# Scores and mix of an attention block by seven half-block products, with sums kept in PSUM

## The chip, the cores and the metric

The kernel runs on one core of a Trainium2 chip. The metric is the device time of one execution in microseconds (us). A core has TensorE (PE; the loads of its weights are shown apart as PEld), VectorE (DVE), ScalarE (ACT), GpSimd (POOL) and SyncE (SP, which only issues transfers). Each engine works through its own queue in order. TensorE writes its results to PSUM, eight banks of 128 x 512 float32.

## The reference, cut to what matters

There are four sequences of 512 tokens by 512 features, all in float32, with full 512 x 512 attention and no mask:

```
q, k, v  = x @ Wq, x @ Wk, x @ Wv
attn     = softmax(q @ k.T * 512**-0.5)
attn_out = (attn @ v) @ Wp + bp
cms      = gelu(attn_out @ cW1 + cb1) @ cW2 + cb2 + one_hot(code)
mod      = gelu(concat(attn_out, cms) @ mW1 + mb1) @ mW2 + mb2
y        = clip(x + cms + mod, 0, 1)
# then, per sequence, an adapter chosen by its stream:
out      = layernorm(y + gelu(y @ Wd + bd) @ Wu + bu) * g + b
```

cW1 is 512 x 2048, mW1 1024 x 2048, cW2 and mW2 2048 x 512, Wd 512 x 256.

## The kernel before

Everything is kept with features (or the summed index) on the 128 partitions. A tile of 512 x 512 is four chunks of 128 x 512. The sequences are worked on in two pairs. First an **attention stage** runs for both pairs; then, for each pair, the layers c1 (cW1), c2 (cW2), m1 (mW1), m2 (mW2) and the adapters follow.

The attention is folded. `block_weights` makes `w_qk` = Wq Wk^T and `w_vp` = Wv Wp once. For a pair, the loop does the following:

- `transposed` turns the rows of x (16 transposes of 128 x 128 on TensorE into four banks) to get `xT`.
- `pair_product` with `w_qk` makes `u` for both sequences at once. It is a Strassen-Winograd product: each operand is cut into four blocks, and seven block products of sums of blocks take the place of eight. The two sequences are the two column blocks of the right operand, so a block product has 512 columns. Each product lands in a bank of its own, and VectorE adds it to the running results in SBUF (`plus`, `add`, line 512).
- `softmax` makes the **scores** of each sequence, `u`^T `xT`, as a plain product: 4 row tiles of 4 chained products of 512 columns (line 596). Per tile VectorE takes the maximum, ScalarE the exponential with its sum, VectorE the reciprocal, ScalarE scales.
- The probabilities are turned (line 414), and `product` makes the **mix** of each sequence, again plain (line 428). `second_operand` forms the sums of blocks that the next pair product needs while it empties the banks.
- `pair_product` with `w_vp` and the bias makes `attn`, which the ACT queue sends to memory (`attn_kept`, line 647).

A float32 product is two matmul instructions in the profile, each with its own weight load.

The operand sums of the weights of c1, c2, m1 and m2 are made by GpSimd during the attention stage and the first c1 layer (`expansion`, called in steps from the loop). The c1 layer takes its seven outer products in the order 2, 1, 5, 6, 7, 3, 4; products 1 and 5 are themselves cut into seven (`inner`, called from `c1_layer`, line 787), with ScalarE copying the first product (line 680) and VectorE doing seven additions into SBUF for each half `g` of the rows (line 673). The weights come over SP's queue (`fetch`, line 762) into four places, `wslot[0]` to `wslot[3]`, taken in turn by `next_weights`. Ahead of them on that queue stands `load_attn` (line 732), which brings the first pair's `attn` back into the slots that held `x_rows[2]` and `x_rows[3]`.

A framework orders the instructions of each engine: by the order of the program, but an instruction whose inputs it takes to be late can be passed by a later one. `keep_in_program_order` forbids that for one instruction. It also hands out the PSUM banks (`bank`, eight in all); a product waits until one is free.

Of the kernel before, what the change touches and what calls it, by code (L numbers as in the profile page):

```python
# [18 lines left out]
def kernel(  # L19
# [452 lines left out]
    transposed(chunks(x_rows[0]), big[2])  # L472
    load_bias()
# [47 lines left out]

    def second_operand(v0, v1, space):


        t12, t34 = (t.rearrange("p (k c) n -> p k c n", k=2) for t in space)
        t1, t2, t3, t4 = t12[:, 0], t12[:, 1], t34[:, 0], t34[:, 1]

        def minus(out_, one, two):
            nc.vector.tensor_tensor(out_, one, two, ALU.subtract)

        def finish(d, ps):
            nc.scalar.copy(v1[:, d, :], ps)
            c = d % 2
            if d < 2:
                minus(t1[:, c], ps, v0[:, c, :])
            else:
                minus(t2[:, c], ps, t1[:, c])
                minus(t3[:, c], ps, v1[:, c, :])
            if d == 3:
                minus(t4, v0[:, 2:4, :], t2)  # L540

        operands = {
            1: v0[:, 0:2, :], 2: v0[:, 2:4, :], 3: v1[:, 2:4, :], 4: t4, 5: t1, 6: t2, 7: t3,
        }
        return operands, finish

    def pair_product(lhs, rhs, out, bias_c=None):

        p5 = [None, None]
        for p in (1, 2, 5, 6, 7, 3, 4):  # L550
            for r in range(2):
                c11, c12, c21, c22 = (out[k][:, o + r, :] for o in (0, 2) for k in range(2))

                def plus(dst, ps, other, o):
                    if bias_c is None:
                        add(dst, ps, other)
                    else:
                        nc.vector.scalar_tensor_tensor(
                            dst, ps, bias_c[:, o + r : o + r + 1], other, ALU.add, ALU.add
                        )  # L560

                ps = bank(f"pair{p}")
                for c in range(2):
                    nc.tensor.matmul(  # L564
                        ps,
                        lhsT=lhs[p][:, c, r * P : (r + 1) * P],
                        rhs=rhs[p][:, c, :],
                        start=(c == 0),
                        stop=(c == 1),
                    )  # L570
                if p == 1:
                    nc.scalar.copy(c11, ps)
                    nc.scalar.copy(c21, ps)
                elif p == 2:
                    plus(c11, ps, c11, 0)
                elif p == 5:
                    p5[r] = ps
                elif p == 6:
                    add(c21, ps, c21)
                    add(c12, p5[r], c21)  # L580
                elif p == 7:
                    plus(c21, ps, c21, 2)
                    add(c22, p5[r], c21)
                elif p == 3:
                    plus(c12, ps, c12, 0)
                else:
                    add(c21, ps, c21)
# [3 lines left out]
    def softmax(k, xT, u):  # L591
        rows = []
        for t in range(NT):
            ps = bank("scores")
            for c in range(NV):
                nc.tensor.matmul(  # L596
                    ps,
                    lhsT=u[:, c, t * P : (t + 1) * P],
                    rhs=xT[:, c, :],
                    start=(c == 0),  # L600
                    stop=(c == NV - 1),
                )
            top = small.tile([P, 1], F32, name="top")
            nc.vector.tensor_reduce(top, ps, AX.X, ALU.max)
            low = small.tile([P, 1], F32, name="low")
# [672 lines left out]
```

## Time and profile before

| | |
|---|---|
| median of three runs | 1213.1 us (1208.37, 1213.10, 1213.13) |
| the profiled execution | 1209.13 us, its span in the trace 1207.3 us |
| attention stage in the trace | 0 to about 264 us |
| first pair's c1 layer | about 264 to 358 us |
| PE busy, share of the span | 1183.2 us, 98% |
| DVE | 866.9 us, 72% |
| ACT | 226.1 us, 19% |
| POOL | 460.8 us, 38% |
| granted TensorE clock | 0.997 of full speed |

How to read the profile: "busy" of an engine is the time in which at least one of its instructions was open. A matmul's duration overlaps that of the next, so its mean duration is longer than its share: the time from one matmul to the next is read from the chain that ended last, where a run of them is one piece with its count. That chain follows the work back from the end, at each step to what released it; the names in it are engine, tile written and line. A group line gives the line, engine, operation, output and inputs, count, busy time, the mean of one in ns, and, after the bar, the idle time of the engine just before these instructions with what ended it.

### The profile page before, as it was taken

The page shows a single profiled execution, that of the slowest core. Times are in us where ns is not written, and L with a number is a line of the kernel's source. Part 1 is how long each engine was busy: PE and PEld are TensorE (multiplying, and loading weights), DVE is VectorE, ACT ScalarE, POOL GpSimd, SP SyncE. Part 2 cuts the span into 40 slices and gives each one's busy share as a digit, 9 for nine tenths or more (in the row PEclk, how much of TensorE's full clock was granted, in tenths as well). Part 3 has the DMA queues.
Part 4 walks back from the last instruction along what each step waited for, and adds up shares of the span by engine and source line. Part 5 has one row for each costly group of instructions (what it writes and reads, how often), then busy time and mean ns, then how long its engine had stood idle before and what let it go on. Part 6 is the DMA issues. An engine that isn't in the chain of part 4 may idle for free.

```text
span 1207.3 us, 12428 instructions
## 1 busy us (share of the span) xinstructions
PE 1183.2 (98%) x4593; PEld 853.5 (71%) x4593; DVE 866.9 (72%) x1156; ACT 226.1 (19%) x383; POOL 460.8 (38%) x501
## 2 busy tenths in 40 slices
PE   8999999999999999989999999999999999999996
PEld 5444454447458888878888857547888888888872
DVE  2542453167979876899799938879895578699947
ACT  3132114104130000003220025332000003230014
POOL 6679999979700028980000443200000010124015
PEclk9999999999999999999999999999999999999998
DMA  9656575797734667876756563233654555674601
GB/s 332 260 192 243 191 298 207 265 372 269 248 118 175 244 227 295 332 277 202 234 204 239 185 226 96 87 106 130 249 169 142 207 183 190 202 252 179 230 1 70
DMA packets 78364, 251.46 MB, mean 208 GB/s; under 512 B 7348, under 2 KB 34016, under 8 KB 63456
## 3 DMA queue, kind: packets, MB, share of 16 engines
q1 hardware_dynamic: 54768, 149.96, 34.9%
q0 software_dynamic: 20736, 89.17, 21.0%
q10 hardware_dynamic: 2800, 11.54, 2.4%
q8 instruction: 36, 0.59, 0.2%
q14 instruction: 24, 0.20, 0.0%
HBM read 185.63 MB, written 65.01 MB: 208 GB/s over the span
## 4 chain that ended last, share of the span: by engine, by line
PE 91%; DVE 4%; issue 3%; POOL 1%; DMA 0%; ACT 0%; ACTq 0%; DVEq 0%; POOLq 0%
PE i L977 28%; PE i L893 26%; PE c L829 11%; PE pair L564 8%; PE prod_ps L428 7%; PE scores L596 5%; PE i L787 2%; PE down_ps L1085 2%; PE tr_ps L414 1%; DVE hidden L512 1%; PE up_ps L1097 1%; DVE slot L190 1%; POOL part L1080 1%; DVE part L673 0%; POOL part L1130 0%
## 5 line engine op out<-in xcount | busy, mean ns | idle before, releaser
L893 PE MATMUL i<-slot,wslot 128*128 128x256 f32 x1184 | 261.6, 379 | 3.8 <-DVE part L673 3.8
L893 PEld LDWEIGHTS i<-slot,wslot 128*128 128x128 f32 x1184 | 224.6, 190 | 35.5 <-DVE part L673 4.1
L977 PE MATMUL i<-slot,wslot 128*128 128x256 f32 x896 | 202.5, 379 | 0.0
L977 PEld LDWEIGHTS i<-slot,wslot 128*128 128x128 f32 x896 | 170.2, 190 | 23.1
L977 PE MATMUL i<-hidden,wslot 128*128 128x256 f32 x576 | 132.2, 379 | 0.0
L680 ACT COPY first<-i 128x256 f32<-128x256 f32 (+1 forms) x56 | 26.8, 478 | 542.3 <-PE i L977 280.6
L673 DVE TENSOR_TENSOR part<-i,part 128x512 f32<-128x512 f32 (+1 forms) x156 | 90.9, 591 | 42.4 <-PE i L893 25.8
L977 PEld LDWEIGHTS i<-hidden,wslot 128*128 128x128 f32 x576 | 109.4, 190 | 16.2 <-issue 1.4
L702 ACT ACTIVATE hidden<-hidden,bias 128x512 f32<-128x512 f32 x128 | 85.2, 714 | 113.9 <-DVE hidden L512 112.0
L829 PE MATMUL c<-slot,wslot 128*128 128x512 f32 x224 | 96.9, 592 | 0.0
L829 PEld LDWEIGHTS c<-slot,wslot 128*128 128x128 f32 x224 | 42.6, 190 | 53.6 <-issue 50.7
L1048 POOL DMA_INDIRECT slot<-in_L_cond_b_up,idx_e x3 | 4.3, 1424 | 187.7 <-PE i L893 187.0
L1048 POOL DMA_INDIRECT slot<-in_L_cond_W_down,idx_d x12 | 15.5, 1291 | 149.8 <-PE i L977 88.6
L673 DVE TENSOR_TENSOR hidden<-i,hidden 128x512 f32<-128x512 f32 x80 | 53.6, 685 | 13.1 <-PE i L893 12.1
L512 DVE TENSOR_TENSOR hidden<-hidden,hidden 128x512 f32<-128x512 f32 (+2 forms) x48 | 58.9, 1231 | 1.2
L284 POOL DMA_DIRECT2D slot<-in_L_cond_mW x24 | 17.9, 761 | 107.6 <-DVE slot L190 106.6
L190 DVE TENSOR_TENSOR slot<-hidden,slot 128x1024 f32<-128x1024 f32 x48 | 58.4, 1218 | 0.3
L190 DVE TENSOR_TENSOR slot<-hidden 128x1024 f32<-128x1024 f32 x48 | 58.4, 1217 | 0.0
L673 DVE TENSOR_TENSOR part<-i,first 128x512 f32<-128x512 f32 (+1 forms) x62 | 36.3, 589 | 27.8 <-PE i L893 15.4
L512 DVE TENSOR_TENSOR hidden<-part,hidden 128x2048 f32<-128x2048 f32 x20 | 55.7, 2784 | 0.5
L512 DVE TENSOR_TENSOR hidden<-c,hidden 128x512 f32<-128x512 f32 x64 | 43.3, 685 | 16.8 <-PE c L829 16.1
L596 PE MATMUL scores<-hidden,hidden 128*128 128x512 f32 x128 | 55.3, 592 | 0.0
(270 smaller groups left out, 1793.6 us busy)
## 6 DMA issues: line engine op xcount, KB each, us to landing
wslot<-m_kept SPq DMA_DIRECT2D x48, 1024.0 KB
wslot<-m_kept SPq DMA_DIRECT2D x36, 512.0 KB
wslot<-c_kept SPq DMA_DIRECT2D x16, 1024.0 KB
slot<-in_L_cond_mW POOLq DMA_DIRECT2D x24, 512.0 KB
wslot<-in_L_cond_mW SPq DMA_DIRECT2D x24, 512.0 KB
slot<-in_L_cond_cW POOLq DMA_DIRECT2D x16, 512.0 KB
wslot<-in_L_cond_cW SPq DMA_DIRECT2D x32, 256.0 KB
m_kept<-wide POOLq DMA_DIRECT2D x6, 1024.0 KB
```

The source lines that it names most:

```text
L190: i = eng.tensor_tensor(out_, one, two, ALU.subtract)
L428: nc.tensor.matmul(ps, lhsT=lhs(c)[:, d * P : (d + 1) * P], rhs=rhs(c), start=(c == 0), stop=(c == 3),)
L512: nc.vector.tensor_tensor(dst, a, b, ALU.add)
L564: nc.tensor.matmul(ps, lhsT=lhs[p][:, c, r * P : (r + 1) * P], rhs=rhs[p][:, c, :], start=(c == 0), stop=(c == 1),)
L596: nc.tensor.matmul(ps, lhsT=u[:, c, t * P : (t + 1) * P], rhs=xT[:, c, :], start=(c == 0), stop=(c == NV - 1),)
L673: nc.vector.tensor_tensor(dst, ps, other, ALU.add)
L680: nc.scalar.copy(c1, p1)
L702: nc.scalar.activation(block[:, t, :], block[:, t, :], AF.Gelu, bias=bias_c[:, 8 * half + t : 8 * half + t + 1],)
L787: nc.tensor.matmul(out_ps[:, j, :], lhsT=a[:, place[q], j * P : (j + 1) * P], rhs=two_level[p][q][:, 0, :], start=True, stop=True,)
L829: nc.tensor.matmul(ps, lhsT=lhs(c, t), rhs=one_level[p][:, c, :], start=(c == 0), stop=(c == 1),)
L893: nc.tensor.matmul(out_ps[:, j, :], lhsT=a[j][q][:, c, :], rhs=now[q][:, c, :], start=(c == 0), stop=(c == 1),)
L977: nc.tensor.matmul(ps[:, :256], lhsT=a[k // 2][q][:, k % 2, :], rhs=now[q][:, k, :], start=(k == 0), stop=(k == 3),)
```

## The change

1. **Scores and mix** become seven block products each (`small_product`): both operands of 512 x 512 are cut into four blocks of 256 x 256, and a block product is 2 row tiles x 2 chunks of 256 columns in one bank.
2. **Sums left in PSUM** (`seven`, used by the scores, the mix, the pair products and the inner products of c1): products 2, 7, 4 and 3 are added by TensorE onto a bank that already holds an earlier product or a sum that VectorE wrote there. Per row tile, ScalarE (for the first mix VectorE) copies product 1 out, VectorE forms 1+5 in SBUF and three sums in PSUM, and ScalarE copies each finished block out; in the pair product with the bias it adds the bias in the same instruction.
3. **Operand sums**: each left operand needs s1 to s4 and each right operand t1 to t4, of 128 x 2 x 256 each. They are made on VectorE, in part while banks are emptied (`right_from_psum`, `beside_u`), in part by pinned instructions called after a given block product (`later`, `then`). They lie in `wslot[0]` to `wslot[2]` and in parts of `big` not in use; `wslot[3]` holds the copies of product 1 and the sums 1+5.
4. **Turning beside products**: the turning of Wv, of both sequences' probabilities and of the second pair's x is issued after a given block product inside another product.
5. The softmax works on 256 rows x 512 keys as two blocks: two maxima of 128 x 2 x 256, one small maximum, four exponentials of 256 columns with their sums, and the scaling. The scale of the maximum moves from VectorE to ScalarE; `constants` moves from behind the weight product of the first pair to behind its last pair product.
6. In the c1 layer, products 1 and 5 take both halves `g` side by side (two weight tiles at once), with their temporaries in `mod[0]`; h11 is added to straight from PSUM, and its eight gelus follow product 5. The generator of the layer pauses 12 times instead of 14.

The diff, cut to its core:

```diff
--- before
+++ after
-    transposed(chunks(x_rows[0]), big[2])
-    load_bias()
...
+        def take(half, at, ps):
+            c, n = at
+            into_ = slice(2 * half + c.start, 2 * half + c.stop)
+            nc.scalar.copy(v1[:, into_, n], ps)
+            if half == 0:
+                minus(t1[:, c, n], ps, v0[:, into_, n])
             else:
-                minus(t2[:, c], ps, t1[:, c])
-                minus(t3[:, c], ps, v1[:, c, :])
-            if d == 3:
-                minus(t4, v0[:, 2:4, :], t2)
+                minus(t2[:, c, n], ps, t1[:, c, n])
+                minus(t3[:, c, n], ps, v1[:, c, n])
+        last = later((t4, v0[:, 2:4, :], t2, ALU.subtract))
...
-    def pair_product(lhs, rhs, out, bias_c=None):
...
+    def seven(rows, matmuls, keep, order, then=None, copy=nc.scalar.copy, at=None):
+        w, x, y, c1, c15 = ([None] * rows for _ in range(5))
+        def space():
+            temps[0] += 1
+            k = temps[0] % 4
+            return wslot[3][:, 512 * k : 512 * k + 512] if at is None else at[:, k, :]
+        for p in order:
+            for r in range(rows):
+                if p in (1, 5, 6):
+                    ps = bank(f"sum{p}")
+                    {1: w, 5: y, 6: x}[p][r] = ps
+                else:
+                    ps = {2: w, 7: x, 4: x, 3: y}[p][r]
+                matmuls(p, r, ps, p in (1, 5, 6))
+                if p == 1:
+                    c1[r] = space()
+                    copy(c1[r], ps)
+                elif p == 5:
+                    c15[r] = space()
+                    add(c15[r], ps, c1[r])
+                elif p == 6:
+                    add(y[r], x[r], c15[r])
+                elif p == 7:
+                    v = bank("sum")
+                    add(v, x[r], c15[r])
+                    keep(r, (1, 1), v)
+                elif p == 2:
+                    keep(r, (0, 0), w[r])
+                elif p == 4:
+                    add(x[r], x[r], c1[r])
+                    keep(r, (1, 0), x[r])
+                else:
+                    keep(r, (0, 1), y[r])
+            for f in then.get(p, ()) if then else ():
+                f()
+    def pair_product(lhs, rhs, out, bias_c=None, beside=None, then=None):
+        def matmuls(p, r, ps, first_):
+            for c in range(2):
+                nc.tensor.matmul(
+                    ps,
+                    lhsT=lhs[p][:, c, r * P : (r + 1) * P],
+                    rhs=rhs[p][:, c, :],
+                    start=(first_ and c == 0),
+                    stop=(c == 1),
+                    skip_group_check=True,
+                )
+        def keep(r, place, ps):
+            o, k = place
+            dst = out[k][:, 2 * o + r, :]
+            if bias_c is None:
+                nc.scalar.copy(dst, ps)
+            else:
+                nc.scalar.activation(dst, ps, AF.Identity, bias=bias_c[:, 2 * o + r : 2 * o + r + 1])
+            if beside is not None:
+                beside(r, place, ps)
+        seven(2, matmuls, keep, (1, 2, 5, 6, 7, 4, 3), then)
...
+    def left_sums(t, s):
+        a11, a12, a21, a22 = halves(t)
+        s1, s2, s3, s4 = (s[:, k] for k in range(4))
+        return later(
+            (s1, a21, a22, ALU.add), (s2, s1, a11, ALU.subtract),
+            (s3, a11, a21, ALU.subtract), (s4, a12, s2, ALU.subtract),
+        )
...
+    def right_from_psum(t, s):
+        t1, t2, t3, t4 = (s[:, k] for k in range(4))
+        def finish(d, ps):
+            nc.scalar.copy(t[:, d, :], ps)
+            c = d % 2
+            if d < 2:
+                minus(t1[:, c], ps[:, 256:], t[:, c, :256])
+            else:
+                minus(t2[:, c], ps[:, 256:], t1[:, c])
+                minus(t3[:, c], ps[:, 256:], t[:, c, 256:])
+                minus(t4[:, c], ps[:, :256], t2[:, c])
+        return finish
+    def small_product(lhs, rhs, keep, then=None, copy=nc.scalar.copy):
+        def matmuls(p, _, ps, first_):
+            v = ps.rearrange("p (j n) -> p j n", j=2)
+            for j in range(2):
...
+        seven(
+            1, matmuls, lambda _, place, ps: keep(*place, ps.rearrange("p (j n) -> p j n", j=2)),
+            (1, 5, 6, 2, 7, 3, 4), then, copy,
+        )
...
+        def keep(half, key_half, ps):
+            got[half, key_half] = ps
+            if (half, 1 - key_half) not in got:
+                return
+            blocks = (got[half, 0], got[half, 1])
+            tops = small.tile([P, 2, 2], F32, name="tops")
+            for i, blk in enumerate(blocks):
+                nc.vector.tensor_reduce(tops[:, :, i], blk, AX.X, ALU.max)
+            top = small.tile([P, 2], F32, name="top")
+            nc.vector.tensor_reduce(top, tops, AX.X, ALU.max)
+            low = small.tile([P, 2], F32, name="low")
+            nc.scalar.activation(low, top, AF.Copy, scale=-SCALE)
+            totals = small.tile([P, 2, 2], F32, name="totals")
+            rows = mod[k][:, 2 * half : 2 * half + 2, :]
...
+    def beside_u(s):
+        s1, s2, s3, s4 = (s[:, k] for k in range(4))
+        def beside(u0):
+            def take(r, place, ps):
+                if place == (0, 0):
+                    minus(s3[:, r], ps[:, :256], u0[:, r, 256:])
+                elif place == (1, 0):
+                    minus(s2[:, r], ps[:, 256:], s3[:, r])
+                    add(s1[:, r], ps[:, 256:], u0[:, r, 256:])
+                    minus(s4[:, r], ps[:, :256], s2[:, r])
...
+    first_operand(0)
+    load_bias()
+    begun = both_operands(0)
...
+        s_u = [sums_in(wslot[k]) for k in range(2)]
+        s_x = [sums_in(wslot[k]) for k in (2, 0)]
+        t_p = t_x
+        operands, last = begun
+        t_x1 = right_sums(xT[1], t_x[1])
+        then = {6: last, 7: t_x1} if pair == 0 else {5: t_x1[:2], 6: last, 7: t_x1[2:]}
+        wv_t = rows_of(wslot[1])
         if pair == 0:
-            transposed(chunks(wv), attn[0])
-            lhs_vp = block_weights(chunks(attn[0]), chunks(wp), w_vp, slot[2])
-            constants()
+            then[7] = [lambda: transposed(chunks(wv), wv_t)] + t_x1
+            then[4] = left_sums(x_rows[0], s_x[0])
+        pair_product(lhs_qk, operands, u, beside=beside_u(s_u[0])(u[0]), then=then)
+        if pair == 0:
+            lhs_vp = block_weights(chunks(wv_t), chunks(wp), w_vp, slot[2])
         steps(expanding, 6)
         pT, mix = u, xT
-        p_rows = [softmax(k, xT[k], u[k]) for k in range(2)]
+        def turn(k):
+            transposed(lambda t: mod[k][:, t, :], pT[k], right_from_psum(pT[k], t_p[k]))
+        s_u1, s_x1 = left_sums(u[1], s_u[1]), left_sums(x_rows[s1], s_x[1])
         for k in range(2):
-            transposed(lambda t: p_rows[k][t], pT[k])
-            finish = into(mix[0])
-            if k:
-                operands, finish = second_operand(*mix, mod)
-            product(chunks(x_rows[s0 + k]), chunks(pT[k]), finish)
+            softmax(
+                k, left_operand(u[k], s_u[k]), right_operand(xT[k], t_x[k]),
+                {6: s_x1[:2], 7: [lambda: turn(0)] + s_x1[2:]} if k else {6: s_u1[:2], 7: s_u1[2:]},
+            )
+        for k in range(2):
+            if k == 0:
+                def keep(half, tokens, ps):
+                    nc.scalar.copy(
+                        mix[0][:, 2 * half : 2 * half + 2, 256 * tokens : 256 * tokens + 256], ps
+                    )
+            else:
+                operands, take, last = second_operand(*mix, mod)
+                held = []
+                def keep(half, tokens, ps):
+                    if (half, tokens) == (1, 1):
+                        held.append(ps)
+                        return
+                    take(half, (slice(0, 2), slice(256 * tokens, 256 * tokens + 256)), ps)
+                    if (half, tokens) == (0, 1):
+                        take(1, (slice(0, 2), slice(256, 512)), held[0])
+            small_product(
+                left_operand(x_rows[s0 + k], s_x[k]), right_operand(pT[k], t_p[k]), keep,
+                {7: [lambda: turn(1)]} if k == 0 else None,
+                nc.scalar.copy if k else nc.vector.tensor_copy,
+            )
             steps(expanding, 6)
-        pair_product(lhs_vp, operands, attn, bp_c)
+        then = {6: last}
+        if pair == 0:
+            begun = []
+            s_next = left_sums(x_rows[2], s_x[0])
+            then = {
+                5: s_next[:2],
+                6: last + [lambda: first_operand(1)],
+                7: s_next[2:],
+                4: [lambda: begun.extend(both_operands(1))],
+            }
+        pair_product(lhs_vp, operands, attn, bp_c, then=then)
+        if pair == 0:
+            constants()
         for k in range(2):
             nc.scalar.dma_start(out=attn_kept[s0 + k], in_=attn[k])
...
+        def matmuls(q, g, ps, first_):
+            for j in range(2):
+                nc.tensor.matmul(
+                    halves_of(ps)[:, j, :],
+                    lhsT=a[g][:, at_[q], j * P : (j + 1) * P],
+                    rhs=rhs[q][:, 0, :],
+                    start=(first_ and j == 0),
+                    stop=True,
+                    skip_group_check=True,
+                )
+        def keep(g, place, ps):
+            o, t = place
+            tiles, tokens = slice(4 * o + 2 * g, 4 * o + 2 * g + 2), slice(256 * t, 256 * t + 256)
+            nc.scalar.copy(h[2 if p == 1 else 3][:, tiles, tokens], halves_of(ps))
+            if p == 1:
+                done = h[0][:, tiles, tokens]
+                add(done, halves_of(ps), done)
+        seven(2, matmuls, keep, (1, 5, 6, 2, 7, 3, 4), at=mod[0])
+        if p == 5:
+            gelu(h[0], 0, cb1_c, range(8))
     def c1_layer(h, rhs, after):
         two_level, one_level, rest = rhs
         for p in FIRST_C:
+            if p in (1, 5):
+                c1_two_level(p, h, two_level[p])
+                yield
+                continue
...
```

## The prediction

> **What bounds the kernel now.** The page's first part, busy time by engine, then the table of stretches (busy time of each engine in a window, in the order PE, PEld, DVE, ACT, POOL, then clock, DMA share, GB/s) for the start, the attention stage and the first c1 layer:
>
> ```profile
> PE 1183.2 (98%) x4593; PEld 853.5 (71%) x4593; DVE 866.9 (72%) x1156; ACT 226.1 (19%) x383; POOL 460.8 (38%) x501
> ...
> 0.00:4.58 4.58, 0.00 (x0) 0.03 (x1) 0.06 (x1) 0.00 (x0) 3.56 (x13) 1.00 0.60 180
> 4.58:265.00 260.42, 257.13 (x724) 124.61 (x725) 103.35 (x197) 58.82 (x111) 222.86 (x270) 1.00 0.70 260
> 265.00:358.00 93.00, 92.55 (x273) 51.48 (x272) 75.28 (x98) 28.26 (x43) 51.25 (x55) 1.00 0.63 231
> ```
>
> After the first 4.58 us, which wait for weights, TensorE is idle for 3.3 us of the attention stage and 0.45 us of c1. VectorE is at 40% and ScalarE at 23% there. So a microsecond taken from TensorE comes off the end, and one added to VectorE costs nothing until TensorE waits for it. The chain that ended last (start, length, engine, tile, line, count) shows both, for the first pair:
>
> ```profile
> 28.11 24.04 PE pair L564 x56
> 52.15 1.43 PE tr_ps L414 x13
> 53.60 0.70 DVE hidden L107
> 54.35 14.00 PE prod_ps L428 x32
> 68.35 27.48 PE scores L596 x64
> 95.86 0.70 DVE top L604
> 96.58 0.16 DVE low L606
> 96.77 0.79 ACT mod L609 x2
> 97.66 0.68 DVE hidden L107
> 98.34 0.14 issue
> 98.48 13.97 PE prod_ps L428 x32
> 112.45 1.43 PE tr_ps L414 x13
> 113.91 0.70 DVE hidden L107
> 114.65 14.00 PE prod_ps L428 x32
> 128.65 24.03 PE pair L564 x56
> ...
> 357.75 84.61 PE i L977 x392
> ```
>
> TensorE pieces follow one another, with short DVE and ACT pieces between them only where something is turned. The last line is the price of a 256-column matmul.
>
> **What the Trainium skill says.** "VectorE: DVE Perf Modes", section "The TRN2 errata", gives a float32 tensor_tensor as (N+151)/0.96 ns, and "Why PSUM operands drop a tier" says that a PSUM operand leaves float32 at one element a cycle. That is 691 ns for 512 and 424 ns for 256; here line 512 takes 690 ns with a PSUM input and the 256-column sums take 0.42 us. "TensorE: Matmul & The Clock Gate", section "Back-to-back issue gap", gives 262 cycles for 256 columns and 518 for 512, so halving costs 1%; here two of 0.2158 (84.61/392) stand against one of 0.4294 (27.48/64), 0.5%. "PSUM — Partial Sum Buffer", section "PSUM bank collisions raise a hardware error", says that accesses of two engines to one bank must be kept apart. The trace agrees: the subtraction of `second_operand` needs no copied value for its first two tiles, yet waits behind ScalarE's copy from the same bank (DVE mod L529 <- ACT hidden L532, 25.1 us in ten waits). So each step of `seven` on a bank is a hand-over, and TensorE takes part in it.
>
> **The change, part by part.**
>
> (a) *Block products.* Scores or mix of one sequence were 16 products = 32 instructions of 512 columns, 32 x 0.4294 = 13.74 us. They become 7 x 4 products = 56 instructions of 256, 56 x 0.2158 = 12.09. Eight times 1.65 is **-13.2 us**, all on TensorE and so on the path. Its bounds: at 0.239 an instruction (line 787, 30.6 us for 128, whose groups of four are often interrupted) a product takes 13.4 and only 2.9 us are won.
>
> (b) *Turning beside products.* Turning stays 16 transposes, 1.75 us each time. What goes is the wait for emptying: from the chain, 54.35 less 52.15 and 1.75 is 0.45 us, and likewise 0.90, 0.45, and 0.53 and 0.45 in the second pair: **-2.8 us** at most. The transposes inside a product need four banks while it holds up to eight. Each of the seven such places may wait for an addition and a copy (0.69 + 0.59), 1.3 us, or be passed by later products: 0 to +9, I take **+1**.
>
> (c) *Pair products.* Still 56 instructions of 512 columns, 24.04 us: 0. VectorE's fourteen additions of 0.69 become eight, and ScalarE gets eight copies of 0.59 in place of four. Hidden under 24 us of TensorE. No row shows VectorE writing PSUM; taken as 0.69 like the reading, between 0.6 and twice that. At twice, 8 x 1.4 = 11 us are still covered.
>
> (d) *Sums and the load on VectorE.* Per pair: sums for u 3.4 (8 x 0.42) and 2.8 (4 of 512 columns at 0.69), for xT 3.4 and 2.8, for x 5.6, for the turned probabilities 6.7; additions of four small products 16 x 0.69 = 11.0; less six additions of each pair product 8.3 and about eight emptying copies 5.5, now on ScalarE. Net +22, for both pairs +44: 147 us of some 250, no bound as a sum. But two scores products with one turning last 2 x 12.09 + 1.75 = 25.9 us, and I count 21 us of VectorE in them. There the order of the queues decides.
>
> (e) *New waits.* Products 2 and 7 accumulate: 2 must wait until product 1 is copied out of its bank, 7 until VectorE has read bank 6. In the second sequence's scores, the copy of product 1 (ready 1.73 us after the first sequence's last product, needed after 5.2) stands on ScalarE behind the first sequence's softmax. One half of that is the small scale 0.2, four exponentials at about 0.45 + 0.19 (half of line 609's 0.69 plus overhead, and its accumulator read), two scalings at 0.73: 4.2 us. The second half can start 2.4 us after the last product (one addition, two maxima, one small one), the first half's scalings go between, and I get the copy done about 7.5 us after it: TensorE waits 2.4. Behind it are this sequence's 1+5, product 7, turning and softmax. The first mix, whose copy is on VectorE, finds there turning, sums and maxima: 0.5 us. So about 3 us per pair, **+6**; 0 if the copies slip ahead, up to 6 per pair if both softmax halves go first (4.1) and the mix waits 2.
>
> (f) *c1.* Its 224 instructions stay. VectorE loses about 7.5 us per pair (28 additions of 0.69 and four of 1.2 become 24 of 0.69), but TensorE is idle there for 0.45 and 0.7 us only: at best -1. Against it: `wslot[3]` is in use until the last pair product, so c1's second tiles (2 MB) start later, at the end of the stage and beside the `attn_kept` writes, where the DMA share is 0.99 or more; and both halves are wanted within 0.9 us, where the second had 6. Also:
>
> ```profile
> ACT hidden L834 <- DMA attn_kept<-hidden: 31.8, 1, 31.8
> ```
>
> ScalarE's first copies of c1 wait until that write lands (276.48), and TensorE needs a bank at 277.76: 1.3 us of slack. -1 to +6; I take **0**. GpSimd, 223 of 260 us busy, ends its expansions at about 325 us, ahead of the layers that read them last: `m1` starts at 442. A stage shorter by 16 us leaves that cover.
>
> (g) *Moved smalls.* `constants` (some 5 us of small VectorE work, at 70 us of the trace) now comes beside the second pair's first product, where VectorE has room: 0. If that cover fails, +1.
>
> Sum: -13.2 - 2.8 + 1 + 6 + 0 = **-9 us**: 1209.13 becomes 1200. The median of the three runs shown is 4.0 higher, which would give 1204. The two lower executions (1208.4, 1209.1) and the two higher (1213.1) lie equally far apart, so I say **1202**.
>
> **Rivals.**
>
> *Full gain.* The waits of (e) and (b) vanish since the order lets the copies pass: -13.2 - 2.8 = -16, 1193 to 1197. For it: ScalarE is busy only 23%, and product 2 or 7 comes a whole block product, 1.73 us, after what it needs. Against it: the count of (e).
>
> *The queues decide (slower).* If VectorE and ScalarE hold the order of the program, the sum of exponentials blocks VectorE before the last addition, and each sequence's maxima and exponentials run one after another: two halves of 4.2 + 1.6 us in front of the next product's copy. Then TensorE waits some 6 us in the second scores, 3 in the first mix and 2 at its turning, 11 per pair: 22 - 16 = +6, 1215 to 1220. The point from which this decides is 16/8 = 2 us of waiting per small product. For it: ScalarE already waits 51.5 us for VectorE's scale (ACT mod L609 <- DVE low L606), and this round trip stays. Against it: before, a tile's whole round trip lay under the 3.4 us of products of the next tile, and TensorE lost nothing to it.
>
> *The start of c1 gives it back.* Late weights or a late `attn_kept` cost 4 to 6 us: about -4, no change. The same result follows if the blocks run at line 787's rate.
>
> *It does not do what it says.* If TensorE could not keep adding where VectorE wrote, the instruction counts and times would be the same; this case needs no time of its own.
>
> **Numbers.** I give the forecast (waits of 3 to 9 us, -6 to -13) 0.53, of which 0.05 falls within the bound; full gain 0.20; c1 or a slow rate 0.12; queues 0.15. A measurement of this kernel can tell 0.5%, 6 us, from no change. Faster 0.68, same 0.17, slower 0.15. The range reaches from below the full gain, 1190, to the near edge of the slow case, 1215.
>
> **What would show it.** Right: scores and mix as 448 instructions of 256 columns, at 0.216 each in the chain; the attention stage ending at about 255 us; DVE near 147 us in it; waits of PE for ScalarE's copy in each second scores product. Wrong in (a): chain pieces of 56 above 12.5 us. Wrong in (e): PE idle in the stage below 6 us in all (then full gain) or above 20 (then queues). Wrong in (f): PE idle between the end of attention and product 6 of c1 above 2 us.

## The result, and the profile after

The change makes the kernel slower: 1218.1 us (median of nine runs, 1214.7 to 1221.8) against 1208.4 for the kernel before in the same comparison (nine runs, 1205.5 to 1213.1). The ratio is 1.0074, 95% interval 1.0052 to 1.0095 (ratios here are formed from all the runs of both kernels, so they differ a little from those of the medians). The forecast was 1202, with a range of 1190 to 1215. The profiled execution took 1217.4 us, with a span of 1215.6 against 1207.3.

The busy times and the table of stretches of the kernel after (columns as before: PE, PEld, DVE, ACT, POOL, granted clock, DMA share, GB/s):

```profile
PE 1177.1 (97%) x4785; PEld 893.0 (73%) x4785; DVE 924.7 (76%) x1222; ACT 274.3 (23%) x503; POOL 460.8 (38%) x501
...
4.58:276.00 271.42, 251.37 (x914) 163.53 (x915) 178.55 (x281) 87.53 (x197) 235.52 (x278) 0.96 0.68 252
276.00:369.00 93.00, 93.00 (x275) 51.99 (x274) 69.42 (x88) 37.44 (x61) 40.52 (x48) 1.00 0.61 222
```

In the attention stage TensorE has 251.4 us of work where it had 257.1, but is now idle for 20 us of it where it was idle for 3.3; and its mean clock is 0.96. VectorE shows 178.6 us where the prediction had counted 147. Pieces of the chain that ended last (start, length, engine, tile, line, count):

```profile
68.76 17.28 PE sum L680 x80
89.04 9.99 DVE wslot L631
100.29 13.48 PE sum L680 x50
115.52 15.11 PE sum L680 x70
...
164.72 4.44 DVE target L492 x2
171.54 4.74 DVE ex L496
181.76 6.38 PE sum L596 x8
...
275.77 13.73 PE c L1043 x32
289.50 24.17 PE sum L992 x112
313.67 54.93 PE c L1043 x128
368.61 84.61 PE i L1191 x392
```

The attention stage ends at 275.77 instead of 264.19, **+11.6 us**. c1 of the first pair takes 92.84 us (275.77 to 368.61) instead of 93.56, -0.7; m1 of the first pair takes 171.2 instead of 174.1, -2.9, a layer that the change doesn't touch. That is +8.0 of the span's +8.3. The block products themselves do what was priced: 15.11/70 = 0.216 an instruction. But single VectorE instructions, 10, 4.4 and 4.7 us long, stand in the chain. The waits of TensorE in the stage (who waited for what: us in all, times, longest):

```profile
PE sum L596 <- DVE sum L510: 9.7, 3, 8.2
PE sum L680 <- DVE sum L510: 8.0, 2, 7.3
```

Two waits, of 7.3 and 8.2 us, make up most of it. After each, TensorE is slow for a while: the 50 instructions at 100.29 take 13.48 us and not 50 x 0.216 = 10.8, the eight of 512 columns at 181.76 take 6.38 and not 8 x 0.429 = 3.4. So two waits of 15.5 us bring 5.6 us of slow work with them, and the smaller waits that the kernel before does not have come to 4.0. Another 0.9 us is lost in the turning of Wq at the very start (5.85 us for 29 transposes instead of 4.93), which the change doesn't touch. With the forecast gain that is -16.0 + 15.5 + 5.6 + 4.0 + 0.9 = +10.0 of the +11.6; the other 1.6 us aren't assigned. The Trainium skill, "TensorE: Matmul & The Clock Gate", "Part 1: The HAM clock gate", says that TensorE's clock is halved after an idle window of about 3.4 us until it has been busy for as long; the granted clock here is 0.60 in the 6.1 us after the first wait and 0.58 in the 6.4 us after the second, which agrees.

The instruction in front of the first wait, on VectorE's timeline (start, length, engine, line, operation, tiles, and in brackets the idle time before it), and GpSimd's timeline beside it:

```profile
86.74 2.23 DVE L631 TENSOR_TENSOR wslot<-hidden 128x512 f32<-128x512 f32 x1
88.89 0.15 DVE L727 RECIPROCAL inv<-total 128x2 f32<-128x2 f32 x1
89.00 10.03 DVE L631 TENSOR_TENSOR wslot<-wslot,hidden 128x512 f32<-128x512 f32 x1
98.95 0.68 DVE L711 TENSOR_REDUCE tops<-sum 128x2 f32<-128x512 f32 x1
99.55 0.68 DVE L510 TENSOR_TENSOR sum<-sum,wslot 128x512 f32<-128x512 f32 x1
```

```profile
89.29 2.38 POOL L298 TENSOR_TENSOR slot<-part,slot 128x1024 f32<-128x1024 f32 x1
91.63 2.35 POOL L298 TENSOR_TENSOR wide<-slot 128x1024 f32<-128x1024 f32 x1
...
97.33 0.71 POOL L179 TENSOR_TENSOR slot<-slot,slot 128x256 f32<-128x256 f32 x1
98.00 0.57 POOL L301 DMA_DIRECT2D c_kept<-wide  x1
```

A sum of 512 columns from SBUF, L631 (`later`), is open for 10.03 us. It ends at 99.03, 1.0 us after GpSimd stops its back-to-back sums to issue a DMA (98.00). Behind it in VectorE's queue stands L510, the addition into the bank that TensorE waits for. Not every sum stretches. Groups of VectorE by form, in the stage (count | busy us, mean ns):

```profile
L510 DVE TENSOR_TENSOR sum<-sum,wslot 128x512 f32<-128x512 f32 x48 | 33.0, 693 | 18.3 <-PE sum L596 10.3 <-PE sum L680 8.0
L631 DVE TENSOR_TENSOR wslot<-wslot,hidden 128x512 f32<-128x512 f32 x4 | 12.9, 3229 | 0.1
L631 DVE TENSOR_TENSOR mod<-hidden,mod 128x1024 f32<-128x1024 f32 x4 | 8.3, 2073 | 0.0
L521 DVE TENSOR_TENSOR mod<-tr_ps,mod 128x512 f32<-128x512 f32 x4 | 2.7, 681 | 0.0
```

With one input in PSUM (`sum`, `tr_ps`) a sum of 512 columns takes 0.675 to 0.70 us each time. With both in SBUF the 32 sums of the same size take from 0.68 to 10.03 us, 1.6 on average; the 3.2 of the row above comes from the one of 10.03. The second wait has the same look: the tiny copies and scalings of `constants` (128 x 4, 0.15 to 0.2 us alone) last from 163.1 to 179.2, with a pair of 4.4 us and a single one of 4.8.

### The profile page after: what moved, and what is told of

Read it like the earlier page. It is cut to its first block, busy times and chain, and to the rows that moved or that the text cites. A ratio compares the mean times of both kernels' runs of the same rounds, so it can differ in the third digit from the quotient of the medians.

```text
span 1215.6 us, 13010 instructions
## 1 busy us (share of the span) xinstructions
PE 1177.1 (97%) x4785; PEld 893.0 (73%) x4785; DVE 924.7 (76%) x1222; ACT 274.3 (23%) x503; POOL 460.8 (38%) x501
## 4 chain that ended last, share of the span: by engine, by line
PE 87%; DVE 8%; DMA 3%; ACT 2%; issue 1%; DVEq 0%; ACTq 0%
PE i L1191 28%; PE i L1107 26%; PE c L1043 11%; PE sum L596 5%; PE sum L680 5%; PE sum L992 3%; DVE wslot L631 2%; PE prod_ps L428 2%; PE down_ps L1299 2%; PE up_ps L1311 2%; PE tr_ps L414 1%; DMA wslot<-in_L_cond_mW 1%; DMA wslot<-m_kept 1%; DVE sum L510 1%; ACT mod L720 1%; PE res_ps L1290 1%
## 5 line engine op out<-in xcount | busy, mean ns | idle before, releaser
L1262 POOL DMA_INDIRECT slot<-in_L_cond_W_down,idx_d x12 | 15.5, 1292 | 149.8 <-PE i L1191 88.5
L510 DVE TENSOR_TENSOR hidden<-c,hidden 128x512 f32<-128x512 f32 x64 | 43.4, 688 | 25.6 <-PE c L1043 24.5
L680 PE MATMUL sum<-hidden,wslot 128*128 128x256 f32 x256 | 58.9, 380 | 0.7 <-DVE inv L727 0.4
L190 DVE TENSOR_TENSOR slot<-hidden 128x1024 f32<-128x1024 f32 x48 | 58.5, 1218 | 0.0
L680 PEld LDWEIGHTS sum<-hidden,wslot 128*128 128x128 f32 x256 | 48.2, 190 | 7.8 <-DVE sum L510 0.8
L510 DVE TENSOR_TENSOR hidden<-part,hidden 128x2048 f32<-128x2048 f32 x20 | 47.9, 2396 | 0.5
L510 DVE TENSOR_TENSOR sum<-sum,wslot 128x512 f32<-128x512 f32 x48 | 33.0, 693 | 18.3 <-PE sum L596 10.3
```

Source lines behind the costliest of these rows:

```text
L190: i = eng.tensor_tensor(out_, one, two, ALU.subtract)
L510: nc.vector.tensor_tensor(dst, a, b, ALU.add)
L680: nc.tensor.matmul(v[:, j, :], lhsT=lhs[p][:, c, j * P : (j + 1) * P], rhs=rhs[p][:, c, :], start=(first_ and j == 0 and c == 0), stop=(c ...
```

## Theories and experiments

**Port theory.** A VectorE instruction with two SBUF inputs, and a small SBUF copy or scaling, stands still while GpSimd runs sums without a pause, and the additions behind it in VectorE's queue are late. The Trainium skill, "SBUF — State Buffer", "Who interferes with whom", says that a VectorE instruction with two SBUF inputs contends with a GpSimd instruction that reads SBUF (not with one that only writes), that copies and scalings can contend as well, and that the one that issues first holds the path that both engines share for its whole instruction, while the other blocks. **Queue theory.** VectorE simply has too much to do, in an order that puts the needed addition last.

**GpSimd's sums become writes.** In the kernel after, and as a control in the kernel before, GpSimd writes constants where it summed weights, so both leave the sums of the weights out. The order of the instructions of TensorE, VectorE and ScalarE in the stage stays, as the traces show.

```diff
+        if writes_only[0]:
+            nc.gpsimd.memset(out_, 0.01)
+            return
         nc.gpsimd.tensor_tensor(out_, a, b, op)
```

> The changed kernel with GpSimd's sums of weights before the second layers of m replaced by memsets of the same tiles (so GpSimd writes but reads nothing, and the weights made there are constants); the order of every other engine's instructions is the same. Port theory: no VectorE sum of 512 columns takes over 0.8 us (the longest was 10.0), the constant work takes 5 us, TensorE is idle for less than 5 us of the attention stage after its start (was about 22), and the stage ends at 253 to 258 us in place of 275.8. Queue theory: VectorE's sums have the same place and number, the stage ends within 3 us of 275.8, and TensorE's two long waits (7.3 and 8.2 us) stay above 4 us each.

> The same replacement (GpSimd writes constants where it summed weights) in the kernel before. Port theory: its few sums in SBUF (2.1 us each where 1.2 is the plain price) become short, but TensorE waits for none of them, so its attention stage ends at 263 to 264.5 us as before (264.2). Queue theory says the same. If this kernel gains as much as the changed one, it is GpSimd's transfers or something else that both share, and the port theory falls.

One execution each: 1188.1 us from the kernel after, 1206.9 from the kernel before. With the change the stage ends at 247.82, 16.4 us before the 264.19 of the kernel before and earlier than the 253 to 258 that was expected. The control ends it at 265.38; its 1.2 us more are all lost in the turning at the start. The same VectorE groups in the first of the two:

```profile
L520 DVE TENSOR_TENSOR sum<-sum,wslot 128x512 f32<-128x512 f32 x48 | 33.4, 697 | 21.4 <-PE sum L606 11.0 <-PE sum L690 10.4
L641 DVE TENSOR_TENSOR mod<-hidden,mod 128x1024 f32<-128x1024 f32 x4 | 4.9, 1216 | 0.0
L641 DVE TENSOR_TENSOR wslot<-wslot,hidden 128x512 f32<-128x512 f32 x4 | 2.8, 692 | 0.1
```

Without GpSimd's reads the SBUF sums take 692 ns instead of 3229, and no queue was reordered. The queue theory falls: the work and its order are the same, and the whole 16 us appear. GpSimd is also less busy here, 142.5 us of the stage instead of 235.5; but 9 of the 36 SBUF sums lie for more than half of their time beside one of its writes, and none is stretched. What speaks without that doubt is the version below in which GpSimd goes on summing.

**`constants` put back** to its old place, in the kernel after; and **`constants` moved late**, as the change does it, in the kernel before, alone. The edit of the second (the first is the reverse):

```diff
-            constants()
...
+        if pair == 0:
+            constants()
```

> The changed kernel with the small constant work put back behind the weight product of the first pair (68 us into the trace, where GpSimd has a gap of 7.5 us); nothing else moves in any queue. Port theory (VectorE instructions with two SBUF operands, or small copies and scalings in SBUF, stand still until GpSimd's run of tensor_tensor pauses; TensorE waits behind them): the 17 us that this work took at 163 to 180 us shrink to 5, TensorE's wait of 8.2 us and its slow restart (2.9 us) go, the attention stage ends at 263 to 267 us in place of 275.8, and the time falls by 8 to 12 us, to about the kernel before. Queue theory (VectorE simply has too much to do between the products, at normal durations): this is 5 us of work that must be done somewhere near; the stage ends at 271 or later and the time falls by at most 4 us.

> The kernel before with only the constant work moved, as the change moves it, behind the first pair's last product. Port theory: it meets GpSimd's dense run there too and takes 8 to 17 us on VectorE in place of 5; but before, TensorE has eight free banks and needs nothing back from VectorE until they are used up, so it waits for at most 4 us and the stage ends at 264 to 268 us. A theory in which this move alone costs the changed kernel its 11 us would have the stage end at 272 or later here as well.

Both expectations were missed. Put back: 1222.8 us, ratio 1.0136 (1.0077 to 1.0195). The wait at 173 us shrank to 2.5, but the later work shifted against GpSimd's, and other sums met it. TensorE waits 5.7 us after the first of these and 9.7 after the second:

```profile
93.75 6.62 DVE L631 TENSOR_TENSOR wslot<-hidden 128x512 f32<-128x512 f32 x1
198.04 12.29 DVE L631 TENSOR_TENSOR wslot<-wslot,hidden 128x512 f32<-128x512 f32 x1
```

So where a stall falls is a matter of where two engines' times meet; moving one piece moves the stall. Moved late in the kernel before, which has none of the new sums: 1222.5 us (one execution). Its stage ends at 278.51, 14.3 us later than without the move, so the rival named there, 272 or later, came true. One of the tiny copies there, and TensorE's timeline:

```profile
154.13 5.45 DVE L489 CAST pos<-pos_i 128x4 f32<-128x4 int32 x1
...
167.01 3.38 PE L564 MATMUL pair<-hidden,cms 128*128 128x512 f32 x4 [10.03 <-DVE hidden L107]
```

Here the emptying copies of the turned x (L107) stand behind the constants. The move that the prediction priced at 0 or +1 costs nearly as much here as the block products were to gain, and it does so without them.

**The c1 layer alone** (`seven` and the two-halves order in products 1 and 5, in the kernel before):

```diff
+    def c1_two_level(p, h, rhs):
+        ...
+                fetch(out=w, in_=c1_inner[5, g])
```

> The kernel before with only the change to the c1 layer (products 1 and 5 with both halves side by side, sums in PSUM). The prediction's own step: TensorE's work is the same and its idle time there 0.45 and 0.7 us, so 0 to -1 us. Rival of late weights: with both tiles of weights wanted at once, TensorE waits 2 to 6 us in c1, and the time rises by as much. In the changed kernel the first c1 layer took 92.8 us against 93.6, so I expect about that here, and a ratio that cannot be told from 1.

1206.7 us, ratio 0.9978 (0.9963 to 0.9992); c1 takes 92.85 us instead of 93.56. A ratio that cannot be told from 1 was expected; it lies just below. The first c1 layer is worth its 0.7 us of idle time, and nothing is late for it; most of the rest lies in m1 in this trace (171.3 us instead of 174.1), of which more below.

**The sums on GpSimd.** If GpSimd makes them itself, they can't contend with it. First the pinned sums (all but t4 of the pair products), then `constants` too, then t4 from its bank as well, on VectorE.

```diff
-            tc.keep_in_program_order(nc.vector.tensor_tensor(*op))
+            tc.keep_in_program_order(nc.gpsimd.tensor_tensor(*op))
...
-        tc.keep_in_program_order(nc.vector.tensor_copy(pos, pos_i))
+        tc.keep_in_program_order(nc.gpsimd.tensor_copy(pos, pos_i))
...
-        last = later((t4, v0[:, 2:4, :], t2, ALU.subtract))
+                minus(ps, ps, t1[:, c, n])
+                nc.scalar.copy(t2[:, c, n], ps)
+                minus(t4[:, c, n], v0[:, into_, n], ps)
```

> The changed kernel with the pinned operand sums of two SBUF inputs (four each for the second x turned, for the second u and for both x of a pair) issued on GpSimd in place of VectorE; t4 of the pair products and the constant work stay on VectorE. Port theory: what stood in front of TensorE in the scores (7.3 us, its slow restart of 2.5, and some 4 us of smaller waits in the second pair) goes; the wait behind the constant work at 173 us stays. The stage ends at 260 to 264 us, the time is 4 to 12 us below the changed kernel. Theory that GpSimd has no room: its sums of weights end after 365 us, or TensorE waits for operand sums from GpSimd, and the time is no better.

> As the kernel with the operand sums on GpSimd, and the constant work on GpSimd too, so that VectorE keeps only t4 of the pair products with two SBUF inputs. Port theory: both long waits of TensorE are gone, the stage ends at 248 to 253 us, TensorE's clock never falls inside it, and the time is 1188 to 1197 us, 1.0 to 1.7% below the kernel before: the 16 us that the block products and the turning were worth. Queue theory: VectorE is relieved of 16 sums a pair of 0.7 us, which frees 22 us in all, but the waits at product 7 stay above 4 us in all four scores products, and the time is above 1203.

> As the one before, and t4 of the pair products is taken from PSUM: VectorE leaves t2 in the bank, ScalarE copies it out, t4 is a block in SBUF less the bank. No operand sum in the stage has two SBUF inputs on VectorE then. Port theory: the remaining waits behind t4 (1.3 us in the changed kernel) go, the stage ends at 247 to 250, the time is within 3 us of the one before it. If the added copies on ScalarE and four more steps on each bank cost something, it is up to 4 us slower than that one.

All three are slower than both kernels, and the gains that the port theory expected of them did not come: 1225.8 us, ratio 1.0137 (1.0089 to 1.0185); 1230.7, 1.0172 (1.0136 to 1.0208); 1236.3, 1.0216 (1.0179 to 1.0253). In the first, TensorE waits 23.2 us, until 194, behind the constants and 6.5 for a sum of GpSimd. With the constants gone from VectorE, only GpSimd is left to wait for; TensorE's waits in the second:

```profile
PE sum L680 <- POOL wslot L631: 34.3, 3, 31.7
```

GpSimd was busy for 235 of 271 us of the stage in the kernel after, and a sum handed to it stands in its queue behind the weights' sums. It is no place for work that TensorE needs soon.

**Every sum from PSUM.** VectorE takes each operand sum of the stage with one input in a bank: from the transposes' banks, from the product's own bank before it is given back, or from a bank that ScalarE fills first. `constants` and the bias go ahead of the first weight product, before GpSimd's sums begin (21.5 us). GpSimd keeps all its sums. (The turned Wv also moves, from `wslot[1]` to `mod[0]`.)

```diff
+    def left_by_bank(t, s):
+        ...
+            ps = bank("left").rearrange("p (j n) -> p j n", j=2)
+            nc.scalar.copy(ps, a21)
+            minus(s3, a11, ps)
+            add(ps, ps, a22)
+            nc.scalar.copy(s1, ps)
+            minus(ps, ps, a11)
+            nc.scalar.copy(s2, ps)
+            minus(s4, a12, ps)
...
+    load_bias()
+    constants()
     lhs_qk = block_weights(chunks(big[4]), chunks(big[5]), w_qk, slot[0])
```

To see what each half of this does, two more kernels take one half each, and a control moves `constants` early in the kernel before.

> The kernel after, with every operand sum of the attention stage taken by VectorE with one input in PSUM (from the transposes' banks, from the products' own banks, or from a bank that ScalarE fills first), and with the small instructions of `constants` ahead of the first weight product, before GpSimd's dense run of sums begins. Port theory (two SBUF inputs on VectorE stand still beside GpSimd's sums): no VectorE instruction of the stage takes over twice its plain time, TensorE waits less than 3 us in the stage after its start, attention ends at 247 to 253 us against 275.8 in the kernel after, and the time is 1190 to 1197, faster than both kernels. Rival (hand-over theory: the additional banks and the copies that ScalarE makes for them cost TensorE as much as the stalls did): the waits of TensorE in the stage come to 6 us or more behind ScalarE or behind banks, and the time is 1205 or above.

> The kernel after, with `constants` and the load of the bias ahead of the first weight product, where GpSimd has not yet begun its dense run; all operand sums stay as they are, from SBUF. Port theory: the wait of 8.2 us at 173 us in the kernel after (with the slow matmuls behind it, some 11 us) goes, but the two-SBUF sums are still there and meet GpSimd's sums wherever their times now fall, so one or two waits of 5 us or more remain: 1200 to 1215. Rival (the sums are cheap and the constants alone are the cost): the waits of TensorE in the stage fall below 3 us and the time is 1190 to 1197, as low as with all sums taken from PSUM.

> The kernel with every operand sum from PSUM, and `constants` put back where the change has them, behind the first output projection. Port theory: the small copies and scalings take some 15 us of VectorE again while GpSimd's run is dense, and the additions for the next product stand behind them, so one wait of TensorE of 6 to 10 us comes back at some 150 to 170 us, with slow matmuls after it: 1197 to 1206. Rival (the small instructions cost only where long sums stand in the queue with them): no wait over 2 us, and the time stays at 1190 +- 3.

> The kernel before with `constants` and the load of the bias ahead of the first weight product, nothing else. In the kernel before no matmul waits for them where they stand, so the port theory says no gain: 1205 to 1211. Rival (an early place of the constants is worth something by itself, and part of the gain of the version with all sums from PSUM comes from there): 1200 or below.

In the table "late" is behind the first pair's last product and "early" ahead of the first weight product; each ratio is against the kernel before in the same comparison. The load of the bias is early in the whole right column and in the last row.

| sums of the stage | `constants` late | `constants` early |
|---|---|---|
| plain products, as in the kernel before | 1222.5 (one execution) | 1206.7, ratio 0.9986 (0.9969 to 1.0002) |
| block products, sums from SBUF | 1218.1, 1.0074 (1.0052 to 1.0095) | 1214.5, 1.0032 (1.0011 to 1.0052) |
| block products, every sum from PSUM | 1199.5, 0.9918 (0.9894 to 0.9943) | **1190.2, 0.9835 (0.9801 to 0.9868)** |

With both, the kernel is 1.65% faster than the one before. In the two traces that is 19.0 us: 14.1 in the stage (which ends at 250.07 in the chain), 0.7 in c1 of the first pair, and 4.3 in m1 of the first pair, which is taken up below. The stage's stretch, and TensorE's waits in it:

```profile
4.58:249.91 245.33, 244.06 (x914) 161.13 (x914) 140.85 (x308) 98.58 (x216) 208.85 (x251) 1.00 0.68 253
```

```profile
PE tr_ps L414 <- DMA wide<-in_L_cond_Wq: 4.4, 1, 4.4
PE sum L691 <- ACT wslot L579: 0.8, 2, 0.4
PE prod_ps L428 <- DVE hidden L107: 0.3, 1, 0.3
```

Beyond the wait for the first weights TensorE waits for 1.1 us in all, VectorE is at 140.9 us, and the clock is full. The reason is to be read in the durations of the sums that replace those of the kernel after (least, median and greatest ns of each form):

```profile
L523 DVE TENSOR_TENSOR mod<-hidden,tr_ps x4: 675/678/687, 36.7 to 154.6; 128x512 f32<-128x512 f32 x4
L523 DVE TENSOR_TENSOR wslot<-slot,left x4: 676/682/689, 125.0 to 209.3; 128x512 f32<-128x512 f32 x4
```

None is stretched, beside the same sums of GpSimd. The hand-over theory, additional banks and copies costing as much as the stalls, falls with 0.8 us of waits behind ScalarE. Each half alone leaves its own stall. With the SBUF sums and early constants, one sum with two SBUF inputs costs a wait:

```profile
200.19 12.41 DVE L633 TENSOR_TENSOR wslot<-wslot,slot 128x512 f32<-128x512 f32 x1
...
213.85 3.78 PE L682 MATMUL sum<-hidden,hidden 128*128 128x256 f32 x8 [10.19 <-DVE sum L512]
```

In that trace c1 of the first pair also takes 97.2 us, with a wait of 2.4 for weights. With the PSUM sums and late constants, one pair of scalings of 5.3 us costs a wait:

```profile
155.59 5.30 DVE L489 TENSOR_SCALAR target<-pos,code 128x4 f32<-128x4 f32 x2
...
167.59 5.22 PE L603 MATMUL sum<-mod,wide 128*128 128x512 f32 x8 [4.48 <-DVE sum L511]
```

That wait was expected to be 6 to 10 us and was 4.5; with the slow matmuls after it the stage ends 6.4 us later (256.46 against 250.07). Another 4.0 us of the difference lie in m1 of the first pair (173.7 against 169.7).

m1, which none of these edits touches, takes from 169.2 to 174.1 us (the kernel before) in the traces of this case. The trace of the kernel before shows what its time goes to:

```profile
503.55 11.66 DVE L512 TENSOR_TENSOR hidden<-part,hidden 128x2048 f32<-128x2048 f32 x1
...
519.73 1.99 PE L893 MATMUL i<-slot,wslot 128*128 128x256 f32 x8 [1.40 <-DVE part L673]
```

A sum of 2048 columns with two SBUF inputs is open for 11.66 us beside GpSimd's sums; with every sum of the stage from PSUM the same sum, in the same layer, took 2.37. TensorE's three waits in this m1, 3.8 us in all, are for VectorE's additions behind such sums. So the kernel before pays for the same effect outside the stage. No run here was aimed at m1, so its share of the 1.65% is not shown to be due to the change.

## Why the prediction was wrong

**(a) Block products: right.** 0.216 us an instruction wherever the clock is full. **(b) Turning beside products: right.** In the kernel after none of the five emptying waits is left; the one wait of the kind in its trace (PE prod_ps L428 <- DVE hidden L107, 0.5 us) stands ahead of the first weight product, where the kernel before has it too. With GpSimd's reads gone, the stage ends 16.4 us earlier than before: the -13.2 and -2.8 of these two steps, and nothing against them.

**(c) Pair products: right.** VectorE's additions into a bank take 0.69 us, as assumed; where nothing stalls, a pair product takes 24.03 us for its 56 instructions.

**(d) Sums and the load on VectorE: this step failed, in its price.** The amount of work was counted well: 147 us forecast, 136.2 where GpSimd only writes and nothing is stretched. But every sum was priced at 0.69 for 512 columns and 0.42 for 256, taken from rows with a PSUM input, and the sums that the change pins have both inputs in SBUF. The trace of before held the warning. In the stage it has one such form, the last sum of `second_operand`, beside one with a PSUM input on the same line (least, median and greatest ns):

```profile
L529 DVE TENSOR_TENSOR mod<-tr_ps,mod x4: 678/678/680, 29.6 to 158.9; 128x512 f32<-128x512 f32 x4
L529 DVE TENSOR_TENSOR mod<-hidden,mod x4: 1314/1842/3364, 32.0 to 242.0; 128x1024 f32<-128x1024 f32 x4
```

The 1024-column SBUF sum takes up to 3.36 us, and 1.22 where GpSimd does not read. "No bound as a sum" answered the wrong question: what decided here was not the total of VectorE, but the longest single instruction ahead of an addition that TensorE needs. One of 10 us cost a wait of 7.3 and 2.7 of slow matmuls.

**(e) New waits: the place was wrong.** +6 was given to the wait for ScalarE's copy of product 1. In the kernel after no wait of the stage ends on ScalarE's copy (one of 0.7 us ends on VectorE's copy in the first mix, priced at 0.5); in the fast version waits for ScalarE's copies are 0.8 us in all. The waits that came were for the additions, 17.7 us in two rows, and with the halved clock after them more than the gain. The softmax round trip on which the "queues decide" rival was built costs next to nothing: with GpSimd's reads gone the same queues lose nothing. That rival's number, 1215 to 1220, fits the measured 1218 by luck: its mechanism was wrong. The prediction's own sign for it, TensorE idle in the stage for more than 20 us, was just reached (20.05) and would have pointed to it.

**(f) The start of c1: right.** -0.7 us, no late weights: both halves' tiles were there. The fear was not idle, though: in three of the other versions TensorE waits 1.2 to 4.4 us in c1 for these weights.

**(g) `constants`: this step failed.** "VectorE has room: 0. If that cover fails, +1." The room was there on average, but 5 us of small instructions became 16 (163.1 to 179.2), and additions for the second pair's first product stood behind them: 8.2 us of waiting and 2.9 of slow matmuls. The test in the kernel before, where the move alone costs some 14 us, says that this step by itself can cancel most of the gain. In the changed kernel an early place brought only some 4 us (1218.1 to 1214.5), since another sum then met GpSimd.

Steps (d) and (g), and with them the waits missed in (e), share one cause, which the prediction did not look for: GpSimd was treated as an engine whose only bearing was when its weights are done. It is busy for 235 of the stage's 271 us, and it decides how long some of VectorE's instructions take.

## What to carry to other kernels

Before you price VectorE work from a row of the trace, check that the inputs lie in the same memories, and what GpSimd does meanwhile: a sum with two SBUF inputs beside a run of GpSimd sums has no price of its own. The longest in the stage stayed open until GpSimd paused. Look at the greatest duration of a form and not only at its mean, and at what stands behind it in the queue. The remedy that worked here was to keep GpSimd's sums and give VectorE one input in PSUM, and to issue small copies where GpSimd is silent.

## What the runs showed of the hardware

- A VectorE sum can be blocked for longer than one instruction of GpSimd. The page on SBUF speaks of a block for the length of the other instruction; here sums of 0.69 us stayed open for 10.03, 12.29 and 12.41 us, across eight, nine and nine GpSimd sums in a row, and ended about 1 us after GpSimd turned to issue a DMA. All three had even begun 0.3 to 0.4 us ahead of the run's first sum, by the profile's starts. The measurement decides: count on the length of the run. Not every pause ends the block: the sum of 11.66 us in m1 stayed open across a DMA issue at 510.09 and ended at 515.21.
- Small SBUF copies and scalings of 128 x 4, 0.15 to 0.2 us alone, were held for up to 7.56 us in the same way (in the first kernel with the operand sums on GpSimd), while sums of 512 columns with a PSUM input stayed between 0.675 and 0.70 us in the kernel after and in the one with every sum from PSUM.
- GpSimd can lose too. In m1 of the kernel before, four of its sums of 256 columns, 0.72 us alone, took 2.76 to 2.79 us beside VectorE's sums of 2048 columns.
- The waits of TensorE of 7.3 and 8.2 us cost 2.7 and 2.9 us more than themselves, in matmuls at a granted clock of about 0.6 on average.
